# Graph-network kernel: when first nodes, cleared sums and picked addresses are worked out, and how the first gather rows are loaded

## The chip, the cores and the metric

One core of a Trainium2 chip runs the whole kernel. The metric is the time of one execution on the device in microseconds (us). A core has five engines with a queue of their own each, in which the instructions run in order: TensorE (PE: matmuls and transposes), VectorE (DVE), ScalarE (ACT), GpSimd (POOL) and SyncE (SP, which here issues DMAs only). ACT and POOL issue DMAs too. Engines wait for one another by semaphores.

## What is computed

A message-passing layer on a graph with 12,500 nodes of 128 features and 412,500 edges, sorted by their destination, then a residual and a layer norm. Cut to what matters here:

```python
f0 = x0 @ W1_0e / sqrt(32); f1 = einsum('nui,uw->nwi', x1, W1_1o) / sqrt(32)
feat0, self0 = f0[:, :32], f0[:, 32:]          # likewise feat1, self1
e0, e1 = feat0[edge_src], feat1[edge_src]      # gather: one row per edge
h = gelu(gelu(edge_scalar_attr @ W_mlp1 / sqrt(8)) @ W_mlp2 / sqrt(64))
w00, w01, w10, w11 = h @ Wp_00, h @ Wp_01, h @ Wp_10, h @ Wp_11
mid0, mid1 = ...                               # products of w, e and edge_attr
n0 = segment_sum(mid0, edge_dst, N) / sqrt(32) # likewise n1
y = cos * self + sin * (n @ W2)
out = layernorm(x + y)
```

## The kernel before

The edges are cut into 806 **runs** of 512 (four columns of 128, `Q = 4`), and four runs make a **chunk** (`CH = 4`). The order of work on PE, ACT, DVE and SP is written out by hand: instructions of an engine run in the order of the code. The kernel has two stages.

*The table stage* (lines 801 to 828) goes over the 25 groups of 512 nodes. For each group SP loads x (L228), PE turns it (L263), ACT copies it out (L264), PE multiplies by the weights `wf` (L270), DVE copies the features to a tile `ft` of three buffers (L273) and ACT's queue stores it to `table` in memory (L236). Other preparations are hung into this loop by the dictionary `extra`: the first 128 runs' rows are made ready in `load_indices(0)`, which reads raw rows from `scratch`, a tile named `acc` (L397).

*The run stage* (lines 829 to 909) is a loop over runs s. For each run POOL gathers rows by indirect DMA into `G` (L197, four gathers of 128 rows at most, 20 buffers). The first 18 runs gather rows of x itself, so that they needn't wait for the table: PE turns them (L541), ACT copies (L543), PE multiplies (L549), ACT copies to `ft` (L551). Later runs gather from the table. Some of a run's columns are not gathered by POOL: DVE and ACT pick them out of `xT` by address (L165, L167; addresses in `pick` tiles), or SP fetches them row by row (L184; addresses in `aid_at`). PE makes the edge weights `w` of two runs at a time (L532), DVE the messages `M` (L574, L577) and the one-hot `pl` (L600), PE the segments (L591), and once per chunk PE places them (L607) and DVE adds them to the sums `acc` at `first_at` (L616). `select` (L559 to L567) makes a chunk's one-hot tile `S`.

Between the stages the code of before does the following on DVE, in this order:

- `aid_load` (L125 to L141): SP issues 13 small loads of row numbers (L128, L137), and DVE turns the numbers into addresses (L129 once, L139 four times).
- `select(0)`.
- `find_first` (L354 to L365): from the first node of every run, loaded in the table stage to `first_node`, it works out where in the sums each run begins. It clears a line of 806 numbers on one partition and then overwrites its tail 24 times (L357, L360), then runs five operations over the line (L361 to L365). Its three lines lie in the three buffers of the message tile `M` (`line`, L288 to L291).
- the clearing of the first sums, a tile of 128 x 3072 (L846). The clearing of the next sums is spread over the runs in four parts (`clear_sums`, L371; list `clearing`, L849).

At the start `load_raw_rows` (L92) loads the row numbers `idx_raw` of the 18 first runs: those of the first two by SP, the rest by ACT's queue behind the first weights.

Of the kernel before, what the change touches and what calls it, by code (L numbers as in the profile page):

```python
# [20 lines left out]
P = 128  # L21
# [31 lines left out]
def gnn_kernel(ctx: ExitStack, tc: tile.TileContext, x, src, dst, ea4, ea8, w1_0, w1_1, wm1, wm2,  # L53
# [38 lines left out]
    def load_raw_rows(eng, a, z):  # L92
        if z == NS and REM < SB:
            z -= 1
            nc.vector.memset(idx_raw[:, z], 0)
            if RQ:
                eng.dma_start(idx_raw[:, z, :RQ], sub(src, z * SB, [[1, P], [P, RQ]]))
            if RP:
                eng.dma_start(idx_raw[:RP, z, RQ:RQ + 1], sub(src, z * SB + RQ * P, [[1, RP], [1, 1]]))
        if z > a:  # L100
            eng.dma_start(idx_raw[:, a:z].rearrange("p s q -> p (s q)"),
                          sub(src, a * SB, [[1, P], [P, (z - a) * Q]]))
# [22 lines left out]
    def aid_load():  # L125


        nc.sync.dma_start(aid_at, sub(src, AID_FROM * SB + (Q - 1) * P, [[AID * SB, len(aided)], [1, P]]))  # L128
        nc.vector.tensor_scalar(aid_at, aid_at, float(4 * P), None, op0=OP.mult)  # L129
        for e, g in picked.items():  # L130
            cycle = CH // math.gcd(CH, COLS[e])
            for h in range(0, len(g), P):
                part = g[h:h + P]
                rows = cst.tile([len(part), P], I32, name=f"pick{len(pick_rows)}")
                for i in range(min(cycle, len(part))):
                    n = len(part[i::cycle])
                    nc.sync.dma_start(rows[i::cycle], sub(src, part[i][2] * SB + COL_Q[e] * P,  # L137
                                                          [[cycle * COLS[e] * SB, n], [1, P]]))
                nc.vector.tensor_scalar(rows, rows, 4.0, float(x_at), op0=OP.mult, op1=OP.add)  # L139
                for i in range(len(part)):  # L140
                    pick_rows[e, h + i] = rows[i:i + 1]  # L141

    picking = {e: [] for e in picked}

# [140 lines left out]
    ones = cst.tile([P, 1], F32)  # L285
    spent = cst.tile([P, 1], F32)

    def line(dtype=F32):  # L288

        t = wk.tile([P, Q, 2, P], F32, name="M", bufs=3)  # L290
        return t.rearrange("p q a k -> p (q a k)").bitcast(dtype)[0:1, :NS]  # L291

    first_node = line(I32)

    w1r = cst.tile([P, HID], F32)
    block = cst.tile([P, 2 * Q], F32)
# [52 lines left out]
    assert all(len(bs) == 1 for c, bs in due.items() if c < NCH - 1)  # L349
    assert N - base[-1] + W <= ACC and ACC - GN <= GN  # L350
    first_at = cst.tile([1, NS], I32)
    assert NS <= Q * 2 * P

    def find_first():  # L354

        floor, strays = line(), line()
        nc.vector.memset(floor, 0.0)  # L357
        for c, bs in due.items():
            if (c + 1) * CH < NS:
                nc.vector.memset(floor[:, (c + 1) * CH:], float((bs[-1] + 1) * GN))  # L360
        nc.vector.tensor_tensor(floor, first_node, floor, op=OP.subtract)  # L361
        nc.vector.tensor_scalar(strays, floor, 0.0, float(ACC - W), op0=OP.max, op1=OP.min)
        nc.vector.tensor_copy(first_at, strays)
        nc.vector.tensor_tensor(strays, strays, floor, op=OP.not_equal)
        nc.vector.tensor_reduce(odd[0:1, 2 * NB:], strays, axis=mybir.AxisListType.X, op=OP.add)  # L365

    def new_sums():
        A["next"] = wk.tile([P, 4, ACC], F32, name="acc")
# [25 lines left out]
        return off  # L394

    raws = {}
    scratch = wk.tile([P, 4, ACC], F32, name="acc")  # L397

    def rows_tile(part=None):

        if part is None:
# [3 lines left out]
    def load_raws(b):  # L405
        raws[b] = [load_run_rows(dst, b, NO_NODE, None if b else 0), load_run_rows(src, b, 0, None if b else 1)]
# [391 lines left out]
            normalise()  # L798

    with tc.manual_schedule(engines={PE, ACT, DVE, SP}):  # L800
        load_raw_rows(nc.sync, 0, min(2, raw_runs))
        load_w1(nc.scalar)
        if raw_runs > 2:
            load_raw_rows(nc.scalar, 2, raw_runs)
        for s in range(min(LEAD - 2, raw_runs)):
            gather(s)
        nc.vector.tensor_scalar(ident, diag, 0.0, None, op0=OP.is_equal)
        for b in range(min(3, NG)):
            XT[b] = load_nodes(b)
        make_wf()  # L810
        clear()
        loads = list(weight_loads())
        extra = {2: lambda: load_edges(0), 3: lambda: load_attributes(0), NG // 2 - 2: lambda: turn_attributes(0), 4: lambda: load_raws(0), NG // 2: lambda: load_indices(0),
                 NG // 2 + 3: make_w1b, NG // 2 + 5: make_ws, NG - 6: lambda: radial(0), NG - 4: lambda: mlp1(0),
                 NG - 2: lambda: mlp2(0), NG - 1: make_wpost}
        for b in range(NG + 2):
            if b < NG:
                turn(b)
            if 0 < b <= NG:
                features_of(b - 1)  # L820
            if 1 < b:
                store_nodes(nc.scalar, table, b - 2, PF[b - 2])
            if b + 3 < NG:
                XT[b + 3] = load_nodes(b + 3)
            if b > 4 and loads:
                nc.sync.dma_start(*loads.pop(0))
            if b in extra:
                extra[b]()
        assert not loads
        for c in range(1, min(EDGES_AHEAD, NCH)):  # L830
            load_edges(c)
        if aided:
            aid_load()
        for s in range(min(LEAD - 2, raw_runs), min(LEAD - 1, NS)):
            gather(s)
        if NCH > 1:
            radial(1)
            mlp1(1)
            mlp2(1)
        weights(0)  # L840
        select(0)
        turn_rows(0)
        features(0)
        find_first()
        new_sums()
        nc.vector.memset(A["next"], 0.0)  # L846
        A["now"] = A["next"]
        new_sums()
        clearing = [(0, a) for a in range(4)]  # L849
        pick_nodes(ACT, 0)  # L850
        for s in range(NCH * CH + CH):
            c, k = divmod(s, CH)
            if s + LEAD - 1 < NS:
                gather(s + LEAD - 1)
            if k == 3 and c + EDGES_AHEAD < NCH:
                load_edges(c + EDGES_AHEAD)
            if s % P == P // 2 - 16 and (s // P + 1) * P < NS:
                load_raws(s // P + 1)
            if s % P == P // 2 and (s // P + 1) * P < NS:
                load_indices(s // P + 1)  # L860
            if s % ET == 8 and s - 8 + ET < NS:
                load_attributes(s // ET + 1)
            for t in range(P // ROWS):
                a = s + AID_LEAD - t * STEPS // (P // ROWS)
                if a in aided:
                    aid(a, t)
            end = c == NCH - 1
            if k % 2 == 0:
                pick(ACT, len(picking[ACT]) // 2)
            if k % 2 == 0 and s + 2 < NS:  # L870
# [12 lines left out]
            if k > 1 and c + 2 < NCH:  # L883
                pick(ACT, P)
                (mlp1 if k == 2 else mlp2)(c + 2)
                if k == 3 and c + 3 == NCH:
                    nc.scalar.activation(spent, ones, AF.Sqrt)
            pick(ACT, P)
            pick_nodes(ACT, s + 1)
            if s + 1 < raw_runs:  # L890
                turn_rows(s + 1)
            if s < NS:
                messages(s)
                placing(s)
                pick_nodes(DVE, s)
                pick(DVE, P)
            if s + 1 < raw_runs:
                features(s + 1)
            if k == (1 if end else 2) and 0 < c <= NCH:
                add(c - 1)  # L900
            if k == (1 if end else 3) and 0 < c <= NCH:
                norm(due.get(c - 1, []), last=c == NCH)
                clearing += [(c, a) for a in range(4)] if c - 1 in due and c < NCH else []
            elif clearing:
                clear_sums(clearing.pop(0)[1])
            if k == 3 and c + 1 < NCH:
                select(c + 1)
            if s == NS - 8:
                count_odd()

# [30 lines left out]
```

## Time and profile before

| what | us |
|---|---|
| median of 3 runs (lowest, highest) | 3654.95 (3654.35, 3660.78) |
| the profiled execution, its own time | 3654.6 |
| its span, from the first to the last instruction | 3652.8 |
| busy in the span: DVE | 3077.8 (84%) |
| POOL | 2736.6 (75%) |
| PE | 2618.5 (72%) |
| ACT | 2391.7 (65%) |

The profile shows one execution. "Busy" leaves out register work and the issue of DMAs, and a POOL instruction of the kind L197 is the making of a gather's descriptors, not the transfer. A row of a timeline gives the start in us, the duration in us, the engine, the line, the operation with the tile it writes and those it reads, and in brackets the engine's idle time before it with what ended it by the profile's reckoning. A group's row gives busy us and mean ns of one, then the idle time before. An x16 means that the row stands for 16 instructions of the kind that follow each other. SPq and ACTq are the DMA issues of those queues. PEclk is the part of full speed that PE's clock was granted.

### The profile page before, as it was taken

What the parts mean: (1) busy time and instruction counts of PE and PEld (TensorE: products, weight loads), DVE (VectorE), ACT (ScalarE), POOL (GpSimd) and SP (SyncE); (2) the same over time, 40 slices, a digit from 0 to 9 for tenths busy, and PEclk for the clock granted to TensorE, in tenths of its full rate; (3) what the DMA queues carried; (4) which work ended last, traced back from release to release, by engine and by line L of the source; (5) the groups of instructions that cost most, each with busy time, mean ns of one, the idle gap of its engine ahead of it and who ended that gap; (6) DMA issues with size and microseconds to landing.
All of it is one profiled execution on the core that took longest, in us unless ns stands there. A gap on an engine that the chain in (4) does not pass through costs nothing.

```text
span 3652.8 us, 129429 instructions
## 1 busy us (share of the span) xinstructions
PE 2618.5 (72%) x29857; PEld 1938.9 (53%) x29857; DVE 3077.8 (84%) x25457; ACT 2391.7 (65%) x18614; POOL 2736.6 (75%) x2887
## 2 busy tenths in 40 slices
PE   5777777877677777677777677677677677677676
PEld 5555555655455555455555455555455555455554
DVE  3688898898898888887887888888888798798886
ACT  2377677677677667666766667666666676676673
POOL 7767777777777777777777777777777777777775
PEclk8989898788888878887788787887887787788877
DMA  9222332333332333322323322223222233233222
GB/s 207 57 57 67 63 63 64 63 63 71 63 63 65 63 63 70 63 62 63 63 59 68 67 60 63 67 60 69 64 62 63 63 63 63 65 63 62 59 64 48
DMA packets 578767, 243.66 MB, mean 67 GB/s; under 512 B 482186, under 2 KB 527072, under 8 KB 577984
## 3 DMA queue, kind: packets, MB, share of 16 engines
q0 software_dynamic: 92160, 188.93, 20.4%
q1 hardware_dynamic: 464542, 39.90, 8.9%
q10 hardware_dynamic: 21282, 6.47, 0.8%
q8 instruction: 238, 3.90, 0.5%
q14 instruction: 545, 4.46, 0.4%
HBM read 222.26 MB, written 12.80 MB: 64 GB/s over the span
## 4 chain that ended last, share of the span: by engine, by line
DVE 31%; issue 16%; POOL 16%; PE 10%; DMA 9%; SPq 7%; ACT 7%; DVEq 4%; ACTq 0%; POOLq 0%
POOL G L197 16%; DVE gt L165 13%; DMA G<-table,idx 8%; DVE M L577 7%; SPq L184 5%; ACT gt L167 3%; DVEq L154 3%; DVE M L574 3%; DVE acc L616 2%; DVE pl L600 2%; PE h L636 2%; PE seg L591 2%; PE w L532 2%; SPq L180 2%; DVE S L567 1%
## 5 line engine op out<-in xcount | busy, mean ns | idle before, releaser
L197 POOL DMA_INDIRECT G<-table,idx x2808 | 2667.1, 950 | 867.8 <-issue 737.2
L167 ACT ACTIVATE gt<-xT 128x1 f32 x16640 | 1664.4, 191 | 146.5 <-issue 144.9
L165 DVE COPY gt<-xT 128x1 f32 x20224 | 1301.6, 145 | 205.0 <-issue 194.2
L532 PE MATMUL w<-wpb,h 64*128 64x128 f32 x6448 | 730.9, 332 | 336.3 <-DVE M L577 334.0
L591 PE MATMUL seg<-M,S 128*32 128x128 f32 x12896 | 652.0, 322 | 419.1 <-DVE M L577 278.5
L532 PEld LDWEIGHTS w<-wpb,h 64*128 64x128 f32 x6448 | 587.5, 226 | 503.9 <-DVE M L577 388.9
L577 DVE TENSOR_TENSOR M<-w,G 128x384 f32<-128x384 f32 x1576 | 797.5, 548 | 0.0
L591 PEld LDWEIGHTS seg<-M,S 128*32 128x32 f32 x12896 | 343.6, 123 | 607.6 <-issue 152.1
L594 ACT ACTIVATE sg<-seg 128x256 f32<-128x256 f32 x403 | 150.9, 374 | 404.0 <-PE seg L591 391.5
L574 DVE TENSOR_TENSOR M<-w,G 128x256 f32<-128x256 f32 x788 | 323.4, 410 | 107.9 <-DMA G<-table,idx 93.7
L515 PE MATMUL h<-h,w2b 64*64 64x256 f32 x3232 | 319.2, 413 | 90.2 <-ACT h L504 87.4
L607 PE MATMUL m<-pl,sg 128*128 128x128 f32 x1612 | 333.0, 370 | 1.5 <-DVE acc L616 0.8
L607 PEld LDWEIGHTS m<-pl,sg 128*128 128x128 f32 x1612 | 282.1, 264 | 59.7 <-issue 57.6
L174 ACT ACTIVATE G<-h 128x128 f32<-128x128 f32 x288 | 79.3, 275 | 331.0 <-PE h L173 293.7
L500 PE MATMUL h<-eT,w1b 64*128 64x128 f32 x3232 | 280.3, 322 | 5.8 <-ACT eT L493 5.8
L500 PEld LDWEIGHTS h<-eT,w1b 64*128 64x128 f32 x3232 | 237.8, 222 | 56.1 <-issue 45.5
L515 PEld LDWEIGHTS h<-h,w2b 64*64 64x64 f32 x3232 | 146.6, 139 | 216.9 <-ACT h L504 177.4
L616 DVE TENSOR_TENSOR acc<-m,acc 128x128 f32 x806 | 234.2, 291 | 30.8 <-issue 2.7
L600 DVE TENSOR_SCALAR pl<-iota,colv 128x128 f32<-128x128 f32 x806 | 241.2, 299 | 5.1 <-PE m L607 5.1
L504 ACT ACTIVATE h<-h 128x512 f32<-128x512 f32 x404 | 215.7, 585 | 35.3 <-PE h L500 33.8
L520 ACT ACTIVATE h<-h 128x512 f32<-128x512 f32 x404 | 214.1, 580 | 19.8 <-PE h L515 14.0
L173 PE MATMUL h<-wf,gt 128*128 128x128 f32 x576 | 146.0, 345 | 14.4 <-ACT eT L493 10.2
(117 smaller groups left out, 1489.8 us busy)
## 6 DMA issues: line engine op xcount, KB each, us to landing
G<-table SPq DMA_DIRECT2D x7040, 0.5 KB
G<-table,idx POOLq DMA_INDIRECT x2808
e<-in_edge_attr SPq DMA_DIRECT2D x201, 64.0 KB
xt<-in_x SPq DMA_DIRECT2D x24, 256.0 KB
table<-ft ACTq DMA_DIRECT2D x24, 256.0 KB
xt<-in_edge_attr SPq DMA_DIRECT2D x24, 256.0 KB
out<-y SPq DMA_DIRECT2D x24, 256.0 KB
xt<-in_dst SPq DMA_DIRECT2D x5, 256.0 KB
```

Of the source, the lines that this page charges most:

```text
L165: nc.vector.tensor_copy(to, col)
L167: nc.scalar.activation(to, col, AF.Copy)
L197: nc.gpsimd.indirect_dma_start(out=G[s][:, q, :], out_offset=None, in_=x if s < raw_runs else table, in_offset=bass.IndirectOffsetOnAxis(a ...
L500: nc.tensor.matmul(p1[h][:, j // 2, j % 2, :], w1b[rows, j, :], eT[c][rows, :], start=True, stop=True)
L515: nc.tensor.matmul(p2[r][k * HID:(k + 1) * HID, h * n:(h + 1) * n], w2b[rows, :], H1[c][h][rows, k * n:(k + 1) * n], start=True, stop=True)
L532: nc.tensor.matmul(WP[i][:, q, :], H2[c][q % 2][rows, k, q // 2, :], wpb[rows, :], start=True, stop=True)
L574: nc.vector.tensor_tensor(m[:, :, :, :MUL], w[:, :, :2 * MUL].rearrange("p q (a u) -> p q a u", a=2), g[:, :, None, :MUL].to_broadcast([P, ...
L577: nc.vector.tensor_tensor(m[:, :, j, MUL:].rearrange("p q (i u) -> p q i u", i=3), w[:, :, None, (2 + j) * MUL:(3 + j) * MUL].to_broadcast ...
L591: nc.tensor.matmul(SEG[c][q * W:(q + 1) * W, r, :], own[:, r * Q + q, col:col + W], M[s][:, q, h, :], start=h == 0, stop=h == 1)
L600: nc.vector.tensor_scalar(PL[s], iota, colv[b][:, r:r + 1], None, op0=OP.is_equal)
L607: nc.tensor.matmul(pt[:, k].rearrange("p a n -> p (a n)"), SG[c][:, k, :], PL[s], start=True, stop=True)
L616: nc.vector.tensor_tensor(a, ST[c][:, k], a, op=OP.add)
```

## The change

Four things are moved or rewritten.

1. The conversions to addresses leave `aid_load` (its DMAs stay where they were) and become a function `addresses`, called after run 1's messages.
2. `find_first` is called there too, behind `addresses`. Its line of steps is no longer made by overwriting tails: each of the 25 pieces is cleared to its own value once. Its three lines lie in `scratch` instead of buffers of `M`; so does `first_node`, whose load by SP now goes to `scratch`.
3. The first sums are cleared in the table stage, at group 13 of 25. The second sums, which take the buffer of `scratch`, are asked for behind `find_first`, and their clearing in four parts falls to runs 2 to 5 instead of 0 to 3.
4. `load_raw_rows` loads the row numbers of three runs by SP, of 15 by ACT's queue.

```diff
-        nc.vector.tensor_scalar(aid_at, aid_at, float(4 * P), None, op0=OP.mult)
...
-                nc.vector.tensor_scalar(rows, rows, 4.0, float(x_at), op0=OP.mult, op1=OP.add)
+                pick_tiles.append(rows)
...
+    pick_tiles = []
+
+    def addresses():
+        nc.vector.tensor_scalar(aid_at, aid_at, float(4 * P), None, op0=OP.mult)
+        for rows in pick_tiles:
+            nc.vector.tensor_scalar(rows, rows, 4.0, float(x_at), op0=OP.mult, op1=OP.add)
...
-    def line(dtype=F32):
-
-        t = wk.tile([P, Q, 2, P], F32, name="M", bufs=3)
-        return t.rearrange("p q a k -> p (q a k)").bitcast(dtype)[0:1, :NS]
-
-    first_node = line(I32)
+    scratch = wk.tile([P, 4, ACC], F32, name="acc")
+    assert 3 * NS <= 4 * ACC
+
+    def line(i, dtype=F32):
+
+        return scratch.rearrange("p a n -> p (a n)").bitcast(dtype)[0:1, i * NS:(i + 1) * NS]
+
+    first_node = line(0, I32)
...
-        floor, strays = line(), line()
-        nc.vector.memset(floor, 0.0)
-        for c, bs in due.items():
-            if (c + 1) * CH < NS:
-                nc.vector.memset(floor[:, (c + 1) * CH:], float((bs[-1] + 1) * GN))
+        floor, strays = line(1), line(2)
+        steps = [(0, 0)] + [((c + 1) * CH, (bs[-1] + 1) * GN) for c, bs in due.items() if (c + 1) * CH < NS]
+        for (r, n0), (z, _) in zip(steps, steps[1:] + [(NS, 0)]):
+            nc.vector.memset(floor[:, r:z], float(n0))
...
-        load_raw_rows(nc.sync, 0, min(2, raw_runs))
+        load_raw_rows(nc.sync, 0, min(3, raw_runs))
         load_w1(nc.scalar)
-        if raw_runs > 2:
-            load_raw_rows(nc.scalar, 2, raw_runs)
+        if raw_runs > 3:
+            load_raw_rows(nc.scalar, 3, raw_runs)
...
         loads = list(weight_loads())
+        new_sums()
...
-                 NG - 2: lambda: mlp2(0), NG - 1: make_wpost}
+                 NG - 2: lambda: mlp2(0), NG - 1: make_wpost,
+                 NG // 2 + 1: lambda: nc.vector.memset(A["next"], 0.0)}
...
-        find_first()
-        new_sums()
-        nc.vector.memset(A["next"], 0.0)
         A["now"] = A["next"]
-        new_sums()
-        clearing = [(0, a) for a in range(4)]
+        clearing = []
         pick_nodes(ACT, 0)
...
+            if s == 1:
+                addresses()
+                find_first()
+                new_sums()
+                clearing = [(0, a) for a in range(4)]
```

More of the change, by code (lines that the diff above doesn't have):

```diff
@@ L351, in gnn_kernel @@
     first_at = cst.tile([1, NS], I32)
-    assert NS <= Q * 2 * P
     def find_first():
-        floor, strays = line(), line()
-        nc.vector.memset(floor, 0.0)
-        for c, bs in due.items():
-            if (c + 1) * CH < NS:
-                nc.vector.memset(floor[:, (c + 1) * CH:], float((bs[-1] + 1) * GN))
+        floor, strays = line(1), line(2)
+        steps = [(0, 0)] + [((c + 1) * CH, (bs[-1] + 1) * GN) for c, bs in due.items() if (c + 1) * CH < NS]
+        for (r, n0), (z, _) in zip(steps, steps[1:] + [(NS, 0)]):
+            nc.vector.memset(floor[:, r:z], float(n0))
         nc.vector.tensor_tensor(floor, first_node, floor, op=OP.subtract)
@@ L396, in gnn_kernel @@
     raws = {}
-    scratch = wk.tile([P, 4, ACC], F32, name="acc")
     def rows_tile(part=None):
```

## The prediction

> **What bounds the kernel now.** I read the groups by cost first, then POOL's own timeline, then the timeline of 84 to 120 us with the PE clock by stretch. The chain of waits comes last and is no guide: it spreads its shares over DVE, "issue" and POOL, because from 207 us on POOL is never late and every other engine works off what it brings.
>
> ```profile
> L197 POOL DMA_INDIRECT G<-table,idx x2808 | 2667.1, 950 | 867.8 <-issue 737.2
> ```
>
> With the 72 gathers of raw rows that makes 2880 gathers, each 0.95 us and then 0.30 us of "issue": one every 1.25 us. 2880 x 1.25 = 3600 of the 3652.8 us. So the span is POOL's stream, plus what POOL waits, plus 22 us after its last gather (start 3629.85). POOL's timeline shows where it waits:
>
> ```profile
> 12.21 0.95 POOL L197 DMA_INDIRECT G<-in_x,idx_raw  x1 [0.30 <-issue]
> 15.88 0.94 POOL L197 DMA_INDIRECT G<-in_x,idx_raw  x1 [2.73 <-DMA idx_raw<-in_src]
> ...
> 188.52 0.94 POOL L197 DMA_INDIRECT G<-table,idx  x1 [3.31 <-PE h L541]
> ...
> 198.72 0.95 POOL L197 DMA_INDIRECT G<-table,idx  x1 [5.51 <-ACT h L504]
> ...
> 206.77 0.94 POOL L197 DMA_INDIRECT G<-table,idx  x1 [0.71 <-DVE M L577]
> ```
>
> Beyond the usual 0.30 it waits 2.43 us at 15.88, and at eight starts from 138 to 207 us 11.3 us in all (0.38, 1.34, 0.56, 0.40, 0.04, 3.01, 5.21, 0.41). After 206.77 no gap exceeds 0.36. The second group is a ring of 20 G buffers running full: the gather for run n needs the buffer of run n-20. The wait at 188.52 (run 37) ends with the turning of run 17, that at 198.72 (run 38) with the messages of run 18 (L577 ends at 197.95; the releaser named is a neighbour), that at 206.77 with those of run 20 (end 206.50). So what counts is **how late the chain PE-ACT-DVE is in the first 20 runs**. Why it is late, in the timeline of all engines:
>
> ```profile
> 85.83 0.35 DVE L139 TENSOR_SCALAR pick<-pick 128x128 int32<-128x128 int32 x2 [0.78 <-DMA pick<-in_src]
> 86.51 0.28 ACT L493 ACTIVATE eT<-h 128x128 f32<-128x128 f32 x1 [6.92 <-DVE oh L559]
> 87.34 0.73 DVE L357 MEMSET M<- 1x806 f32 x1
> ...
> 95.19 5.25 DVE L360 MEMSET M<- 1x470 f32 x15 [0.15 <-DVE M L360]
> 96.80 0.60 ACT L551 ACTIVATE ft<-h 128x512 f32<-128x512 f32 x1 [1.25 <-PE h L549]
> 100.43 0.60 ACT L551 ACTIVATE ft<-h 128x512 f32<-128x512 f32 x1 [1.25 <-PE h L549]
> 100.47 0.99 DVE L361 TENSOR_TENSOR M<-M 1x806 f32<-1x806 int32 x1
> 103.73 0.98 DVE L365 TENSOR_REDUCE odd<-M 1x1 f32<-1x806 f32 x1
> 105.30 2.62 DVE L846 MEMSET acc<- 128x3072 f32 x1 [0.59 <-DVE odd L365]
> 107.85 0.35 DVE L574 TENSOR_TENSOR M<-w,ft 128x256 f32<-128x256 f32 x1
> 108.71 1.12 PE L591 MATMUL seg<-M,S 128*32 128x128 f32 x16 [8.32 <-DVE M L577]
> ```
>
> Features of run 0 are ready at 97.40 and of run 1 at 101.03, but DVE works on first nodes and clearing until 107.9, and PE stands 8.32 us. The windows (columns: stretch, PE, PEld, DVE, ACT, POOL busy, PE clock, DMA share, GB/s) show what that costs besides:
>
> ```profile
> 100.00:105.00 5.00, 0.40 (x4) 0.20 (x2) 4.37 (x8) 0.60 (x1) 3.86 (x4) 0.98 0.21 52
> 105.00:110.00 5.00, 1.29 (x17) 0.65 (x18) 4.65 (x7) 0.00 (x0) 3.77 (x4) 0.50 0.21 52
> 115.00:120.00 5.00, 3.51 (x51) 2.77 (x48) 1.39 (x4) 2.07 (x4) 3.77 (x4) 1.00 0.20 52
> ```
>
> **Part 1, the blocks taken off the way of run 0.** The picked addresses end at 86.2, then S, then first nodes from 87.34 to 104.7, then 2.62 for the sums. In the changed kernel only selecting S precedes the messages of run 0. ACT's eT at 86.51 doesn't come earlier: ACT had just issued the last table store (85.88 to 86.46), which no step here moves, and "oh L559" is only named as neighbour. PE and ACT go on from there as before, at the 0.50 to 0.55 clock of 84 to 95 us, so messages of run 0 start at about 97.5 instead of 107.85, and those of run 1, held by its features, at 101.06; with the placing they end at 102.6 (messages to end of placing took 1.5 in the runs of before).
>
> **Part 2, the block between runs 1 and 2.** (a) Addresses: five operations, 0.22+0.21+0.25+0.35 = 1.0 us; their data landed by 85.8. (b) Clears: before, 25 overlapping ones took 87.34 to 100.44 = 13.1 us, each with a wait for the one before. Now 25 pieces of 6 to 40 elements that don't overlap and, in the compiled stream, don't wait. The 1x38 clear took 90 ns, the 1x6 one 63: 25 x 0.09 = 2.3; if each paid the 0.1 gap of the small ones, 4.8. I take 2.3, since no wait is there. (c) The five lines on 806 elements: 0.99+0.57+0.58+0.99+0.98 plus gaps, 100.47 to 104.71 = 4.25; some 0.2 for the last result. Sum 7.8: messages of run 2 start at 110.4 (before 114.31). Behind the block on DVE wait those messages, on PE the segments of run 2, and the rest of its queue.
>
> **Part 3, where PE stands then.** PE ends the features of run 1 at 100.4. To the segments of run 2 it has, at full clock, segments 0 (0.64), turning 2 (0.66) with ACT's copy and features 2 (1.16), weights (1.16), then the stretch that took 115.33 to 120.30 (4.97) before: it arrives at 109.75. The messages of run 2 let it start 0.86 after their begin (as 107.85 to 108.71), at 111.3; before it was 120.30. **Shift 9.0 us.** From there PE's path is as before (a run each 4.84 us), and DVE has room: it waited 0.4 to 5 us for ft in runs 3 to 17, so the clears that fall at runs 4 and 5 now (0.48 each) hide there.
>
> The Trainium skill, "TensorE: Matmul & The Clock Gate" (Part 1), says that an idle window of about 3.4 us drops the PE to half its clock. The row agrees for the long gap (8.32 us idle, then 0.50), and it decides the sum: four groups after it took 1.12, 1.12, 2.08, 1.83 where the warm ones take 0.64, 0.66, 1.16, 1.16, 2.5 us in all. By the rule the gap that is left (109.75 to 111.3, 1.6 us) keeps the clock: shift 9.0. The trace also has 0.83 at 180 to 190 us with gaps of no more than 1.3; if the short gap cools as the long one did, the shift is 6.5. I take the rule, as the 100 to 105 stretch holds 0.98 well into its idle time.
>
> A rule against the change: "SBUF — State Buffer" (Who interferes with whom) says that DVE's copies, casts and tensor_scalars in a two-port mode shut GpSimd out for their whole length. By it addresses, bounds and cast (1.0+0.57+0.58) would hold POOL 2.2 us. The rows: the gather beside 85.83 took 1.16 instead of 0.94, that of 101.23 1.05, so 0.33 together, and these operations ran beside gathers before too. I take 0; either falls into a wait that POOL has anyway (part 5).
>
> **Part 4, the table stage.** Clearing the sums (2.62) now stands after the copy of 49.99: the next copies (51.48, 52.81, then w1b and 55.40) start 1.8, 1.2 and 0.3 late, their stores too. PE's next loads are asked for when tiles are turned, and these turnings are held 0.25 at most; the turning at 59.94 waits for a load asked at 51.91. DMA is full there (share 1.0 to 1.2 in 50 to 75 us), so bytes, not this order, set its end. The load of first nodes now lands in the scratch, after the cast at 46.17 that reads it; SP asks at 52.37 only, so no wait. I take 0, between -1 and +2.6 (the whole clearing).
>
> **Part 5, three runs' rows first.** SP's first load has 12 columns instead of 8. Eight took 2.6 us from issue to POOL's start, so half more of its part lies between 0 and 1.3; I take 0.4 later. The 2.43 at 15.88 goes: 12 gathers end at 18.7 and the rest landed by 15.9. POOL then arrives at run 38 at 198.72 - 2.43 - 10.94 + 0.4 = 185.8, but its buffer comes free at 198.72 - 9.0 = 189.7. So POOL still waits some 4 us, and **this gain is lost in that wait**; what remains is the shift alone, through the wait of 206.77 too.
>
> **Sum.** 3654.6 (the profiled execution) - 9.0 = 3645.6. The median of the runs is 3654.95, 0.35 above it: 3645.9 us.
>
> **Rivals.** *A smaller gain*: the clears pay their gaps (2.5 more), or the short idle time cools PE (2.5), or the table ends 2.6 later. Shift 4 to 6.5: 3648.5 to 3651. For it: small steps at 180 to 195 run slow without a long gap. Against: no waits in the compiled clears. *POOL alone bounds*: the chain comes 13.3 us earlier and only 0.4 is paid: 3654.95 - 2.43 - 11.3 + 0.4 = 3641.6. It needs more than PE's own limit of 120.30 - 109.75 = 10.5; the slow clock from 182 to 195 would have to vanish as well. *Slower*: the clearing in the table's loop. The copies pass through three ft buffers, each waiting for its store's landing (4.39 us at 60.49). If the 2.62 is paid anew at every return of a buffer, the 12 groups left give four returns, 10.5 us, and ACT's eT and all behind it follow: 3654.95 + 1.5 = 3656.5. It decides from a delay of 9.0 us on. Against it: after 55.40 the delay is down to 0.3. *Not as said*: if run 1's messages waited too, the block would lie before run 0 again, 7.8 instead of 20.5 us; the order of the stream excludes it.
>
> **Numbers.** Forecast 0.63 (3644 to 3648), smaller gain 0.22, POOL alone 0.09, slower 0.06. A change under 0.2% (7.3 us) can't be told from none here: a shift under 7.3 counts as same, which takes the smaller gain and a little of the forecast. Range 3641.5 to 3651. Faster 0.70, same 0.25, slower 0.05.
>
> **What would show it.** Messages of run 0 near 97.5, of run 2 near 110.4; PE's clock 1.0 from 100 to 120; no POOL wait near 16; the wait before run 38 about 4 us, its start near 190; the last gather near 3621. Wrong it would be with eT past 89, or a clear that takes 0.2 each, or a PE clock of 0.5 behind run 2.

## The result, and the profile after

| | before | after |
|---|---|---|
| median of 11 runs each, us | 3657.5 (3654.1 to 3660.78) | 3644.73 (3642.47 to 3650.1) |
| ratio, 95% interval | | 0.997 (0.9962 to 0.9978) |
| the profiled execution, its own time | 3654.6 | 3642.47 |
| its span | 3652.8 | 3640.7 |
| first gather's start | 3.33 | 3.75 |
| POOL's waits beyond 0.30, sum | 13.74 | 0.41 |
| last gather's start | 3629.85 | 3618.1 |

The changed kernel is 0.3% faster, some 11 us by the interval's middle (8 to 14). The profiled executions differ by 12.1 us, and POOL's timeline has nearly all of it: the waits go from 13.74 to 0.41 (13.33 less), the first gather starts 0.42 later, the gathers themselves take about 1.2 more, what follows the last one takes 0.35 less: -13.33 + 0.42 + 1.16 - 0.35 = -12.1.

The changed kernel's groups by cost: the stream of gathers is what it was.

```profile
L203 POOL DMA_INDIRECT G<-table,idx x2808 | 2668.7, 950 | 856.8 <-issue 728.3
```

Its POOL timeline, at the places where the kernel before waited (start, duration, in brackets the idle time before). The gather at 13.90 is the first of run 2, which stood at 15.88 behind a wait of 2.73. The one at 185.81 is the first of run 38, which stood at 198.72 behind a wait of 5.51. The one at 193.71, of run 40, is the only late one that is left:

```profile
3.75 1.10 POOL L203 DMA_INDIRECT G<-in_x,idx_raw  x1 [2.15 <-DMA idx_raw<-in_src]
...
13.90 0.94 POOL L203 DMA_INDIRECT G<-in_x,idx_raw  x1 [0.30 <-issue]
...
185.81 0.94 POOL L203 DMA_INDIRECT G<-table,idx  x1 [0.31 <-issue]
...
193.71 0.94 POOL L203 DMA_INDIRECT G<-table,idx  x1 [0.71 <-DVE M L581]
```

Rows of the changed kernel's timeline of all engines, around the block that was moved. `eT` at 84.80, edge attributes that PE has turned and ACT copies out, is ACT's first work behind the last table store; PE and ACT go on from it to run 0, so it marks the end of the table stage:

```profile
84.80 0.28 ACT L497 ACTIVATE eT<-h 128x128 f32<-128x128 f32 x1 [6.47 <-DMA table<-ft]
95.25 0.42 DVE L578 TENSOR_TENSOR M<-w,ft 128x256 f32<-128x256 f32 x1 [13.94 <-ACT ft L555]
100.35 0.21 DVE L145 TENSOR_SCALAR aid_at<-aid_at 55x128 int32<-55x128 int32 x1
100.48 0.62 DVE L147 TENSOR_SCALAR pick<-pick 128x128 int32<-128x128 int32 x4
101.05 1.06 DVE L366 MEMSET acc<- 1x40 f32 x25
102.15 0.99 DVE L367 TENSOR_TENSOR acc<-acc 1x806 f32<-1x806 int32 x1
106.32 0.40 DVE L578 TENSOR_TENSOR M<-w,ft 128x256 f32<-128x256 f32 x1
107.24 0.89 PE L595 MATMUL seg<-M,S 128*32 128x128 f32 x16
```

DVE now waits 13.94 us for the features of run 0 instead of PE waiting 8.32 us for DVE. The block between runs 1 and 2 lasts from 100.35 to 106.32, and the last row, the segments of run 2, has no bracket: PE doesn't stand in front of them. (Its 16 matmuls take 0.89 instead of 0.65, since the second half waits 0.30 for the rest of the messages.) It came there at 107.24, 0.92 after the messages had begun. Before it was 120.30: a shift of 13.06 us. The windows (stretch; PE, PEld, DVE, ACT, POOL busy; PE clock; DMA share; GB/s) show the clock full where it had been 0.50:

```profile
100.00:105.00 5.00, 4.19 (x58) 3.56 (x59) 4.86 (x36) 1.92 (x5) 4.05 (x4) 1.00 0.21 53
105.00:110.00 5.00, 3.52 (x45) 2.09 (x44) 4.86 (x12) 2.15 (x5) 3.78 (x5) 1.00 0.22 52
```

What became shorter in the block are the 25 clears. One line of code each, in both kernels (count: shortest, median and longest in ns, first and last start in us, the commonest shapes; the first clear of before, 1x806, has a code line of its own):

```profile
L360 DVE MEMSET M<- x24: 63/380/697, 88.3 to 100.4; 1x766 f32 x1, 1x734 f32 x1, 1x702 f32 x1, 1x666 f32 x1
L366 DVE MEMSET acc<- x25: 63/85/92, 101.0 to 102.1; 1x32 f32 x17, 1x36 f32 x6, 1x40 f32 x1, 1x6 f32 x1
```

Before, the clears wrote 10,074 elements where the line has 806: of their 13.1 us, 9.9 is the clears themselves and 3.2 the idle time between them. Now each element is written once; a piece still takes 85 ns, but the next one starts 42 ns after it, so the pieces overlap in time and all 25 are done in 1.06.

The shift arrives whole at the ring of G buffers. The messages of run 18, which held run 38's gather until 197.95, end at 184.94 in the changed kernel. POOL could take that buffer 0.77 later, as before, at 185.71; it comes at 185.81 and finds it free, with 0.1 to spare. Those of run 20 end at 193.44 instead of 206.50, and there POOL, which could start at 193.30, waits 0.41.

### The profile page after: what moved, and what is told of

It is laid out like the page before. It is cut to its first block, busy times and chain, and to the rows that moved or that the text cites. A ratio compares the mean times of both kernels' runs of the same rounds, so it can differ in the third digit from the quotient of the medians.

```text
span 3640.7 us, 129428 instructions
## 1 busy us (share of the span) xinstructions
PE 2642.6 (73%) x29857; PEld 1955.0 (54%) x29857; DVE 3066.8 (84%) x25457; ACT 2392.0 (66%) x18614; POOL 2737.8 (75%) x2887
## 4 chain that ended last, share of the span: by engine, by line
DVE 31%; issue 15%; POOL 13%; PE 11%; DMA 10%; SPq 10%; ACT 6%; DVEq 4%; ACTq 0%; POOLq 0%
DVE gt L171 13%; POOL G L203 13%; DMA G<-table,idx 8%; DVE M L581 7%; SPq L190 7%; DVEq L160 3%; DVE M L578 3%; PE h L640 2%; ACT gt L173 2%; SPq L186 2%; DVE acc L620 2%; DVE pl L604 2%; PE seg L595 2%; PE w L536 2%; DVE S L571 1%
## 5 line engine op out<-in xcount | busy, mean ns | idle before, releaser
L519 PE MATMUL h<-h,w2b 64*64 64x256 f32 x3232 | 331.5, 426 | 99.2 <-ACT h L508 95.3
```

Source lines behind the costliest of these rows:

```text
L519: nc.tensor.matmul(p2[r][k * HID:(k + 1) * HID, h * n:(h + 1) * n], w2b[rows, :], H1[c][h][rows, k * n:(k + 1) * n], start=True, stop=True)
```

## The experiments

The theory: POOL's stream of gathers plus its waits makes the time; in the first 20 runs POOL waits for the chain PE-ACT-DVE; what made the chain late is the length of DVE's block. The rivals: that it is the place of the block (in front of run 0), that it is the third run's rows, or that one of the other engines bounds the kernel. The runs came in three sets, each on a chip of its own, with runs of the kernel before among them: their median was 3657.17 in the first set, 3661.09 in the second and 5681.5 in the third, which is told of at the end. Ratios are against the runs of before of the same set.

**Three runs' rows alone**, put into the kernel before:

```diff
-        load_raw_rows(nc.sync, 0, min(2, raw_runs))
+        load_raw_rows(nc.sync, 0, min(3, raw_runs))
...
-        if raw_runs > 2:
-            load_raw_rows(nc.scalar, 2, raw_runs)
+        if raw_runs > 3:
+            load_raw_rows(nc.scalar, 3, raw_runs)
```

> The kernel before with one part alone: the row numbers of three runs asked for first. Theory of the ring (POOL waits for G buffers because the chain PE-ACT-DVE is late in the first 20 runs, and only its lateness counts): POOL's wait of 2.43 us near 16 us goes, its first gather starts 0.4 us later, and the waits from 138 to 207 us grow by about 2 us, so the last gather stays within 0.6 us of 3629.85 and the time within 1 us of before. Rival (parts add up): the last gather comes 2.0 us earlier, near 3627.8.

Measured: 3657.17 us (3655.02 to 3662.54), ratio 1.0003 (0.9994 to 1.0012): nothing. POOL's timeline of this kernel says why:

```profile
13.84 0.95 POOL L197 DMA_INDIRECT G<-in_x,idx_raw  x1 [0.30 <-issue]
...
122.69 0.94 POOL L197 DMA_INDIRECT G<-table,idx  x1 [5.15 <-PE h L541]
...
199.90 0.94 POOL L197 DMA_INDIRECT G<-table,idx  x1 [4.27 <-ACT h L504]
```

The wait at 15.88 is gone, and POOL runs full into the ring earlier: the sum of its waits is 14.42 us against 13.74. The gather of run 38 starts at 199.90 against 198.72, 1.18 later, and the messages of run 18 begin at 197.79 against 196.61, also 1.18 later. Their start moves with the messages and not with the front of the stream. What was gained at 16 us was given back in the ring. The expectation for the last gather, within 0.6 us of 3629.85, missed: it starts at 3636.46. This profile is of the slowest of the 11 runs (3662.54); its gathers take 5.7 us more in sum than those of before, and its eT came 2.96 later.

**The changed kernel with two runs' rows first**, the same edit the other way round:

```diff
-        load_raw_rows(nc.sync, 0, min(3, raw_runs))
+        load_raw_rows(nc.sync, 0, min(2, raw_runs))
...
-        if raw_runs > 3:
-            load_raw_rows(nc.scalar, 3, raw_runs)
+        if raw_runs > 2:
+            load_raw_rows(nc.scalar, 2, raw_runs)
```

> The changed kernel without that part: two runs first. Theory of the ring: the chain is no longer late, POOL has no wait left to lose time in, so the wait of about 2.4 us near 16 us comes back and costs 2.0 us in full: last gather near 3620.1 instead of 3618.1, unless the chain was itself 0.4 us late (wait of 0.41 at 193.7 us), then 1.6. Rival (that part is worth nothing in either kernel): last gather at 3618.1.

Measured: 3647.81 us (3646.3 to 3651.13), ratio 0.9977 (0.9968 to 0.9987). The interval overlaps that of the changed kernel (0.9962 to 0.9978), so the third run's rows are worth between nothing and some us there. POOL's timeline has its one wait in front again, and none later:

```profile
14.68 0.94 POOL L203 DMA_INDIRECT G<-in_x,idx_raw  x1 [1.23 <-DMA idx_raw<-in_src]
```

It is 0.93 beyond the usual 0.30, where the profile of before had 2.43. The landing of these rows varies from one execution to the next, and the 2.43 on which the prediction counted was a large one. Against the 0.41 of the changed kernel and a first gather 0.16 later, the third run is worth 0.93 - 0.41 - 0.16 = 0.36 us in the profiles. The last gather, expected near 3620.1, starts at 3622.34; 4.1 us of its distance from 3618.1 are longer gathers in that profile.

**The pieces alone**: the kernel before, with the line of steps cleared piece by piece and nothing else.

```diff
-        nc.vector.memset(floor, 0.0)
-        for c, bs in due.items():
-            if (c + 1) * CH < NS:
-                nc.vector.memset(floor[:, (c + 1) * CH:], float((bs[-1] + 1) * GN))
+        steps = [(0, 0)] + [((c + 1) * CH, (bs[-1] + 1) * GN) for c, bs in due.items() if (c + 1) * CH < NS]
+        for (r, n0), (z, _) in zip(steps, steps[1:] + [(NS, 0)]):
+            nc.vector.memset(floor[:, r:z], float(n0))
```

> The kernel before, everything where it was, only the 25 clears of the line of first nodes made as pieces that don't overlap. Theory (the length of the block counts, not its place): clears take 1.1 us instead of 13.1, DVE is done with all its blocks 12 us earlier, near 95.9, before the features of run 0 are ready (97.4); messages of run 0 start near 97.5, PE never stands, POOL waits at 16 us only. Last gather near 3620.5 (3629.85 less 11.3, plus up to 2), time 9 to 10 us below before. Rival (the moves behind run 1 and into the table count): messages of run 0 no earlier than 103, gain under 5 us.

Measured: 3647.35 us (3645.23 to 3650.12), ratio 0.9977 (0.9967 to 0.9986). One edit of four lines gives, within the interval, what the whole change gives. DVE's timeline of this kernel:

```profile
87.32 0.61 DVE L566 TENSOR_TENSOR S<-oh,e 128x384 f32<-128x384 f32 x1
87.88 1.07 DVE L359 MEMSET M<- 1x40 f32 x25
...
93.81 2.62 DVE L845 MEMSET acc<- 128x3072 f32 x1 [0.59 <-issue]
97.87 0.42 DVE L573 TENSOR_TENSOR M<-w,ft 128x256 f32<-128x256 f32 x1 [1.44 <-ACT ft L550]
```

The clears take 1.07 us instead of 13.1. With that, first nodes and the sums' clearing end at 96.43, while the features of run 0 are ready at 97.84: the block lies in front of run 0 as before, and DVE still waits 1.44 for ACT. Moving a block that is hidden already takes nothing more off the path. POOL's only wait is 0.93 at 14.70; those from 138 to 207 are gone.

**The pieces with three runs' rows**, the first and the third of these edits together in the kernel before:

```diff
-        load_raw_rows(nc.sync, 0, min(2, raw_runs))
+        load_raw_rows(nc.sync, 0, min(3, raw_runs))
...
-            if (c + 1) * CH < NS:
-                nc.vector.memset(floor[:, (c + 1) * CH:], float((bs[-1] + 1) * GN))
...
+        for (r, n0), (z, _) in zip(steps, steps[1:] + [(NS, 0)]):
+            nc.vector.memset(floor[:, r:z], float(n0))
```

> The kernel before with the pieces and with three runs' rows first; nothing is moved behind run 1 or into the table. Theory: the same as the whole change, last gather within 1 us of 3618.1, time within 1.5 us of the changed kernel. Rival: the moves carry part of the gain, and this one is 3 us or more behind the changed kernel.

Measured: 3647.61 us (3645.63 to 3651.92), ratio 0.9975 (0.9966 to 0.9984): the same as the pieces alone. POOL's wait at 14.7 is replaced by 0.94 at 188.38 and 0.41 at 196.42; the last gather starts at 3621.82 in the one and 3621.83 in the other. So here the wait in front was taken away and came back in the ring. That is 3.7 after the changed kernel's 3618.1, where within 1 was expected; 2.9 of it are longer gathers in this profile and 0.9 the wait at 188.38.

**The moves without the pieces**: the changed kernel, with the pieces taken back to overlapping tails, the block still behind run 1:

```diff
-        steps = [(0, 0)] + [((c + 1) * CH, (bs[-1] + 1) * GN) for c, bs in due.items() if (c + 1) * CH < NS]
-        for (r, n0), (z, _) in zip(steps, steps[1:] + [(NS, 0)]):
-            nc.vector.memset(floor[:, r:z], float(n0))
+        nc.vector.memset(floor, 0.0)
+        for c, bs in due.items():
+            if (c + 1) * CH < NS:
+                nc.vector.memset(floor[:, (c + 1) * CH:], float((bs[-1] + 1) * GN))
```

> The changed kernel, its order kept, but the line of first nodes cleared by 25 overlapping tails as before. Theory (length of the block counts): the clears take 13.1 us instead of 1.1, messages of run 2 start near 118.3 instead of 106.3, PE stands some 11 us before the segments of run 2 and is granted half its clock after it; the chain is 11 to 13.5 us later than in the changed kernel and POOL pays it less the slack it has, so the last gather comes near 3629 to 3632 and the time is that of before within 3 us. Rival (the place behind run 1 hides the block): time within 3 us of the changed kernel.

Measured: 3663.84 us (3654.05 to 3667.86), ratio 1.0006 (0.9997 to 1.0015): nothing is left of the gain. DVE's timeline of this kernel:

```profile
102.61 0.73 DVE L364 MEMSET acc<- 1x806 f32 x1
103.56 0.70 DVE L367 MEMSET acc<- 1x766 f32 x1 [0.21 <-DVE acc L364]
...
110.45 5.24 DVE L367 MEMSET acc<- 1x470 f32 x15
115.72 0.99 DVE L368 TENSOR_TENSOR acc<-acc 1x806 f32<-1x806 int32 x1
119.89 0.40 DVE L579 TENSOR_TENSOR M<-w,ft 128x256 f32<-128x256 f32 x1
```

The clears take 102.61 to 115.72, 13.1 us again, and between them is idle time that ended with the clear before (the bracket names its line). Now they stand between runs 1 and 2, and PE's timeline shows where the wait has gone:

```profile
120.82 1.12 PE L596 MATMUL seg<-M,S 128*32 128x128 f32 x16 [12.13 <-DVE M L582]
```

PE stands 12.13 us, and its first matmuls after that take 1.12 where warm ones take 0.65. The segments of run 2 start at 120.82, against 120.30 before. So the length of the block decides and not its place: a long one only moves the stall from run 0 to run 2. The profiled execution, 3654.05, is the shortest of the 11 by 7 us (the others take 3661.3 and more), so its last gather, 3628.84 (3629 to 3632 was expected), is that of an execution faster than most.

**Addresses and sums in front again**: the changed kernel with two of the moves undone; pieces and first nodes behind run 1 stay.

```diff
-                 NG // 2 + 1: lambda: nc.vector.memset(A["next"], 0.0)}
...
+        addresses()
         select(0)
...
+        nc.vector.memset(A["next"], 0.0)
         A["now"] = A["next"]
...
-                addresses()
```

> The changed kernel with the addresses and the first sums' clearing put back in front of run 0; first nodes stay behind run 1, pieces and three runs stay. Theory: DVE stood 13.9 us before the messages of run 0 there, so both hide: messages of run 0 within 1 us of 95.25, last gather within 1 us of 3618.1. The end of the table stage (eT of chunk 1 at 84.8 in the changed kernel, 86.5 before) tells whether the clearing in the table loop moved it: if so eT goes back to about 86.5. Rival (these two moves carry part of the gain): last gather 2 to 4 us later.

Measured: 3650.93 us (3649.43 to 3652.97), ratio 0.997 (0.9958 to 0.9982), the same as the changed kernel's. In its DVE timeline the clearing is hidden too:

```profile
88.41 2.62 DVE L850 MEMSET acc<- 128x3072 f32 x1 [0.59 <-issue]
98.07 0.42 DVE L578 TENSOR_TENSOR M<-w,ft 128x256 f32<-128x256 f32 x1 [7.04 <-ACT ft L555]
```

After it DVE has 7.04 us to wait, so these two moves take nothing off DVE's path, and the time shows no loss. The last gather, however, expected within 1 us of 3618.1, starts at 3625.43. By the two profiles, 5.7 of these 7.3 us are longer gathers and 1.4 is a wait at run 38, since the chain is 2.8 later at run 2; 2.1 of that is a later eT (86.90 instead of 84.80).

Counted from eT, the ten kernels of the result and of the first two sets fall into two groups. With pieces, the segments of run 2 start 22.2 to 23.2 us after eT, whether the block lies in front of run 0 (22.7, 23.2) or all or part of it behind run 1 (22.2 to 23.2). With tails they start 33.8 to 34.8 us after it, in front (33.8, 34.8) or behind (34.6).

**More for SP to fetch**: the changed kernel with every 12th run's last column fetched row by row by SP instead of every 14th.

```diff
-AID = 14
+AID = 12
```

> The changed kernel with SP fetching the fourth column of every 12th run instead of every 14th (65 runs instead of 55): 10 gathers fewer for POOL. Theory (the span is POOL's stream alone now): 10 x 1.25 = 12.5 us faster than the changed kernel, if SP's queue can carry it. Rival (another engine or SP bounds as soon as POOL is relieved): under 5 us gained, or slower, with POOL waits of over 0.36 us in the middle of the span.

Measured: 3835.66 us (3831.61 to 3837.13), ratio 1.0472 (1.0458 to 1.0486). Ten gathers fewer, and 4.7% slower. In this kernel's groups by cost PE's turning of edge attributes, which come by SP's queue like these rows, waits for its data:

```profile
L495 PE MATMUL h<-ident,e 128*128 128x128 f32 x202 | 79.1, 392 | 481.1 <-DMA e<-in_edge_attr 475.6
```

POOL waits 117 us in 49 places, 47 of them from 967 us on, as the rival said. SP's queue looks like the next bound, though no run takes work off it to show so: the chain of waits gives it 24% here and 10% in the changed kernel, and after POOL's last gather another 100 us follow (3730.68 to 3831.1) instead of 22.6.

**More for ACT to pick**: the changed kernel with ACT picking a column of every 5th run instead of every 6th.

```diff
-COLS = {DVE: 5, ACT: 6}
+COLS = {DVE: 5, ACT: 5}
```

> The changed kernel with ACT picking a column in every 5th run instead of every 6th: 27 gathers fewer for POOL. Theory (POOL's stream alone): 27 x 1.25 = 34 us faster. Rival (ACT, then PE and DVE behind it, become the bound): ACT gets 27 x 128 x 0.19 = 660 us more work on 2392, the chain falls behind and POOL waits for buffers in the middle of the span; gain under 10 us, or slower.

Measured: 3622.13 us (3618.43 to 3625.75), ratio 0.989 (0.9874 to 0.9905), the fastest of all. 26 gathers fewer (27 were expected) at 1.25 us are 32.5 us; against the kernel with two moves undone, in the same set, it is 28.8 us faster. ACT pays with 2678.5 us busy instead of 2392.0. In POOL's timeline of this kernel a wait of 3.35 is back:

```profile
188.48 0.94 POOL L203 DMA_INDIRECT G<-table,idx  x1 [3.65 <-ACT h L508]
```

Fewer gathers pay in full only while the chain keeps up. That POOL's stream is the bound is shown by this run: work taken off POOL shortens the span, although ACT and PE have more of it.

**A third set, on another chip.** It was to tell whether clearing the sums in the table's loop moves the end of the table, and whether ACT's picks pay in the kernel before. The first, in the kernel before:

```diff
         loads = list(weight_loads())
+        new_sums()
...
-                 NG - 2: lambda: mlp2(0), NG - 1: make_wpost}
+                 NG - 2: lambda: mlp2(0), NG - 1: make_wpost,
+                 NG // 2 + 1: lambda: nc.vector.memset(A["next"], 0.0)}
...
-        new_sums()
-        nc.vector.memset(A["next"], 0.0)
         A["now"] = A["next"]
```

> The kernel before, only the first sums' clearing moved into the table stage. Theory: DVE's block before run 0 is 3.2 us shorter (2.62 and the gap of 0.59 before it), messages of run 0 start that much after eT sooner: 18.1 us after eT instead of 21.3; the chain and so the last gather come 3 us earlier. The five profiles so far of kernels with the clearing in the table show eT at 83.7 to 87.5, the five without at 86.5 to 89.5; if the clearing itself moves the table's end, eT lies below 86 here and the gain is near 5. Rival (the late copies and stores behind the clearing hold the table's end up): eT above 87.5, and no gain.

The kernel before and the changed kernel, each once more and without an edit, beside it:

> The kernel before once more, for one more profile: how far eT, POOL's waits and POOL's busy time differ between two executions of the same kernel. Theory: eT within 1.5 us of 86.51, waits within 2 us of 13.7 in all, the same eight places. If eT differs by more, the 1.7 us between before and after say nothing of the change.

> The changed kernel once more: eT within 1.5 us of 84.80, POOL's waits beyond the usual gap under 3 us in all after its first gather.

And ACT's picks in the kernel before:

```diff
-COLS = {DVE: 5, ACT: 6}
+COLS = {DVE: 5, ACT: 5}
```

> The kernel before with ACT picking a column in every 5th run. Theory: the gain of fewer gathers stands by itself, some 8 ns per thousand of time or 29 us below before, and the 10 us of the change come on top of it only in the changed kernel; so this is near 3633 where before is at 3657. Rival: without the change the late chain takes it, gain under 10 us.

Measured: on this chip every kernel is slower by more than half. The kernel before has a median of 5681.5 us (17 runs, 5659 to 5703) and 5687.11 in the profiled execution; the sums' clearing 5685.72 (5671.41 to 5703.53), ratio 1.0011 (0.9993 to 1.003); the changed kernel 5683.27, one run and no faster; ACT's picks 5801.02 (5780.66 to 5813.43), ratio 1.0206 (1.0178 to 1.0235). In the groups by cost of the kernel before on this chip the instructions of POOL and DVE have their usual lengths, a gather 946 ns and a copy 146, but the engines stand in front of them (PE's matmuls are longer, at a granted clock of 0.66 over the span instead of 0.83):

```profile
L197 POOL DMA_INDIRECT G<-table,idx x2808 | 2656.7, 946 | 2837.7 <-DVE M L577 1140.4 <-issue 1000.5 <-ACT gt L167 266.2
L165 DVE COPY gt<-xT 128x1 f32 x20224 | 1423.4, 146 | 1177.7 <-issue 1158.9 <-DMA G<-table 1.2 <-DMA G<-table,idx 0.6
```

DVE stands 1177.7 us in front of its copies, 1158.9 of them on "issue", where the profile of before has 205.0 in all, and POOL waits 1140.4 us for DVE's messages. POOL is not the bound here, so what is taken off it brings nothing, and what is put on ACT costs 2%. What held the engines up these traces don't show. One expectation held: with the sums cleared in the table, the messages of run 0 start 18.2 us after eT instead of 21.2. The question of the table stays open: the last eT of the table stage (86.51 in the profile of before) came at 154.10 with the clearing in the loop and at 154.22 without, but at 160.69 in the changed kernel, and this table stage isn't that of the other chips, so the two repeats settle nothing.

## Why the prediction was right, and where it wasn't

**What bounds the kernel** was right: POOL's stream, made longer by the ring. The last gather moved from 3629.85 to 3618.1 (3621 was predicted) and the time with it; taking gathers away shortens it further; three runs' rows alone give nothing.

**The size of the shift was too small**, 9.0 against 13.06, and these terms make nearly all of the 4.06:

| term | predicted | measured | us |
|---|---|---|---|
| eT | 86.51 | 84.80 | 1.71 |
| eT to messages of run 0 | 11.0 (the clock as before) | 10.45 | 0.54 |
| addresses | 1.0 | 0.70 | 0.30 |
| 25 clears | 25 x 0.09 = 2.3 | 1.06 in all, 1.1 to the next row | 1.2 |
| five lines and the last result | 4.45 | 4.17 | 0.28 |

The largest term is not in DVE's block but ahead of it. Whether the change brought the 1.71 of eT stays open: in the five kernels outside the third set that clear the sums in the table, it comes at 84.80, 83.69, 86.22, 86.38 and 87.50, in the five that don't at 86.51, 89.47, 87.14, 87.97 and 86.90. The means are 1.9 apart, but each group spreads over 3 to 4 us, and on the chip of the second set the one without the clearing (86.90) lies among the three with it. The prediction took 0, "between -1 and +2.6": too narrow below. The clears: 0.09 is how long one takes, and that was right (85 ns; 2.1 us in sum). But the prediction added the lengths up, and clears that don't wait overlap in time, one every 42 ns. And of the 13.1 us, given as clears "each with a wait for the one before", three quarters was the clears themselves.

**"PE's own limit"** held in its construction: from the segments of run 0 to those of run 2 PE needed 9.10 us (9.35 was predicted). But it was hung on the eT and on the clock of the execution of before, so 109.75 was no limit; PE came at 107.24. The gap of 1.6 us that was to be left, and whether it would cool PE, never arose. The rule of the Trainium skill, "TensorE: Matmul & The Clock Gate" (Part 1), on which the sum rested, agrees with the long gap of the moves without the pieces: after 12.13 us idle the first 16 matmuls took 1.12 instead of 0.65. As the prediction used it, for idle windows, it doesn't cover the half clock further on, of which more below.

**The step that failed** is "this gain is lost in that wait". POOL comes to run 38 at 185.81, as predicted (185.8), but its buffer is free by then (185.71 and not 189.7), since the shift was 13.06. So the wait in front counts, as far as it is there, and no wait of 4 us stands before run 38. The reasoning was sound, as the pieces with three runs' rows show, where the wait did move into the ring; the size of the shift was wrong. That the shift sufficed by 0.1 us is luck, as far as it rests on the 1.71 of eT: without them POOL would have waited some 1.6 us at run 38 (an estimate from these figures). What was measured is nearly the rival "POOL alone bounds": 3641.6 was its time, 3642.47 the profiled execution of the changed kernel. It was given 0.09 for the reason that the slow clock from 182 to 195 would have to vanish as well. It didn't have to. In both kernels that stretch, from the messages of run 15 to those of run 18, took 17.57 us at a mean clock of 0.81. The shift alone was enough.

**The median** was forecast as 3645.9 and came out as 3644.73, nearer than the profiled executions (3645.6 and 3642.47). That is luck, since two things offset each other: the three runs of before on which the forecast rests lie low (3654.95, in 11 runs 3657.5), and the changed kernel's profiled execution was the shortest of its 11.

**The costs put at nothing**: the operations that the rule names did not hold POOL up noticeably. Beside addresses, bounds and cast the gathers took 1.04, 0.94, 1.33 and 0.94, so 0.5 us in all over the usual length, within the 2.2 by the rule and near the 0.33 by the rows. The reason given, that it falls into a wait which POOL has anyway, fails: POOL had 0.41 of waiting left. The clears of the second sums at runs 2 to 5 (0.48 each) hide: from the segments of run 2 to those of run 5 PE took 14.48 us (107.24 to 121.72), and 14.44 before (120.30 to 134.74).

**The rivals**: the slower one, a delay in the table's loop of 9 us, did not come. The smaller gain did not either, but its reason, a slow clock in small steps without a long gap, is real: no idle time of PE within the stretches below exceeds 1.3 us. One stretch of the same 147 matmul groups, from the messages of run 15 to those of run 18, in three kernels' windows: the pieces alone, the changed kernel with two moves undone, and the changed kernel.

```profile
168.60:183.38 14.78, 11.58 (x147) 8.98 (x146) 10.70 (x95) 9.61 (x66) 11.12 (x13) 1.00 0.22 55
```

```profile
168.80:185.18 16.38, 12.84 (x147) 9.91 (x146) 10.69 (x95) 10.22 (x73) 12.41 (x14) 0.90 0.28 56
```

```profile
166.03:183.60 17.57, 14.35 (x147) 11.16 (x146) 10.86 (x96) 10.01 (x69) 13.29 (x15) 0.81 0.27 58
```

At a mean clock of 1.00, 0.90 and 0.81 it takes 14.78, 16.38 and 17.57 us. These are means of full and half: three windows of 3.41 us in the changed kernel's stretch read as follows, two of them at half clock. The kernel with two moves undone has one such half window (177.79 to 181.21), the pieces alone none.

```profile
170.25:173.66 3.41, 3.41 (x37) 2.85 (x35) 2.35 (x11) 1.52 (x11) 2.49 (x4) 0.50 0.17 43
173.66:177.07 3.41, 1.94 (x19) 1.33 (x12) 1.27 (x21) 2.24 (x14) 2.50 (x3) 1.00 0.21 59
177.07:180.49 3.42, 3.42 (x28) 2.78 (x27) 1.70 (x4) 2.33 (x21) 2.80 (x3) 0.50 0.21 59
```

How many there are doesn't follow the edits. In the ten profiles of before, after and the first two sets, the granted clock is 1.00 or 0.50 and changes only at instants that lie whole multiples of 3.41 us apart, and these instants fall differently against the program in each execution. Counted from the last such instant, the messages of run 15 start at 1.11 to 1.24 us in the three profiles with one half window, at 1.33 to 2.27 in the three with none, and at 2.48 to 2.88 in the four with two. So in all ten the offset goes with the number, be it the kernel before or a changed one. That the offset is the cause is inferred: no run sets it. What within a window brings the half clock stays open too: PE is busy 1.43 to 1.95 us of the window in front of each half one, but in two profiles such a window (1.83, 1.71) was followed by a full one.

This is why the pieces alone suffice in their profile: their shift at run 2 is 10.45 us (eT came 2.34 later than in the changed kernel), less than the 12.2 by which POOL comes earlier to run 38 there (waits of 10.94 from 138 us to run 38, 1.50 less in front, a first gather 0.27 later). The full clock adds 2.8 by run 18, whose messages begin at 183.38 against 183.60 in the changed kernel. It also fits three others: the pieces with three runs' rows, the kernel with two moves undone and the one with ACT's picks have shifts of 9.2, 10.3 and 11.3 us, a mean clock of 0.90, 0.90 and 0.82, and 0.94, 1.36 and 3.35 us of waiting at run 38. The 2.6 us by which the changed kernel's shift exceeds that of the pieces alone are 2.34 of eT and 0.27 of the rest. So beside the pieces the moves bring little but what the clearing in the table may take off eT, and no timing here resolves that.

Single profiles have a limit besides: the sum of POOL's busy time over the same 2880 gathers differs by 7 us among the profiles of the eight kernels that make them outside the third set (POOL busy 2736.4 to 2743.5 us). Differences of a few us in the last gather between two profiles are not the edits' alone.

## What to carry to other kernels

Ask first why a block is long, and then where it should stand: 25 overlapping clears wrote twelve times the elements that were needed and waited for each other, and the same result from pieces that don't overlap cost a twelfth, which hid the block where it was. Short instructions that don't wait can overlap in time, so price a row of them by the distance of their starts and not by their lengths. When a producer runs ahead through a ring of buffers, its wait in front and its waits later are the same microseconds: a cut in front pays only once the chain that frees the buffers is ahead too, so work out both arrivals at the buffer that binds, the producer's and the consumer's. Where a sum hangs on the start of a stage in one profiled execution, give that start the spread that other profiles have, 3 to 4 us here, before calling anything built on it a limit.

## What the runs showed of the hardware

- Clears of about 32 elements on one partition: 85 ns each, and where none waits the next starts after 42 ns (25 in 1.06 us). A clear of 806 elements takes 0.73 us, and 0.95 with the idle time behind it where the next one overlaps it; 25 such clears, ever shorter, took 13.1 us.
- The granted PE clock was full or half, in steps of 3.41 us, in ten profiles of nearly the same program. One and the same stretch of instructions had none, one or two half windows and took 14.8, 16.3 to 16.4, or 17.6 to 18.6 us, with no idle time of PE over 1.3 us in the three profiles shown. The number went with where the steps fell against the program, in ten of ten.
- On one chip the same kernel took 5687 us instead of 3655, with single instructions of POOL and DVE as long as elsewhere and idle time on "issue" between them. There the kernel has another bound, and what helped elsewhere brought nothing.
- SP's queue of single rows had no room for ten columns more in this kernel: they cost 4.7%.
